# A four-layer graph network on one core: layer 3's features turned by DRAM, layer 2's by VectorE and ScalarE, in a newly searched order

## The chip, the cores and the metric

The kernel runs on one core of a Trainium2 chip. Its time is the device time of the whole execution in microseconds (us). The profile is one execution, recorded by the hardware profiler.

## What is computed

There are 32 graphs of 512 nodes with 256 features each. Each graph goes through four layers; after each layer the input is added and every node's row is normalised:

```python
x = _layernorm(x + _L0_gnn_ref(x, adj, ...))      # relu((x*(1+eps) + adj @ x) @ W1 + b1) @ W2 + b2
x = _layernorm(x + _L1_gnn_ref(x, adj, ...))      # 4-head attention, edges adj > 0.5
x = _layernorm(x + _L2_gnn_ref(x, adj, ...))      # 8-head attention, scores + log(adj + 1e-6)
x = _layernorm(x + _L3_gnn_ref(x, nodemask, adj, W))
...
# layer 2
q, k, v = split_heads(x @ Wq.T), split_heads(x @ Wk.T), split_heads(x @ Wv.T)
# layer 3
intermediate = einsum('bsh,hd->bsd', matrix, W)
similarities = einsum('bsd,btd->bst', intermediate, matrix) * adj
attn = softmax(where(mask, similarities, NEG_INF)); output = einsum('bst,bth->bsh', attn, matrix)
```

All is float32. A product on TensorE needs the contracted index on the partitions. The normalised x of a layer has nodes on the partitions, so before layers 1, 2 and 3 it has to be turned to features on the partitions: 512 x 256 becomes two tiles of 128 features x 512 nodes. This turning is what the change is about.

## The kernel before

One graph is cut into steps (some 300), each given with an engine, a planned cost in us, the steps it follows, and the buffers it takes. `Plan.order` (L134) lays the steps of up to six graphs into one order, by a due time for each step (its graph's turn, less the work that follows it, plus a shift by the step's name) and by the planned costs; `Plan.run` then emits them in that order. The order is thus fixed when the kernel is built: every engine executes its own instructions in that order and waits by semaphores. The shifts, the period and the window stand in one long list of numbers in the call of `plan.run`. Buffers come from numbered stocks: "B" 13 tiles of 128 x 2048, "C" 12 of 128 x 1024, "D" 10 of 128 x 512, and "p" the 8 banks of PSUM.

The steps that matter here, by their names in the code and the lines of the profile of before:

- **Adjacency.** For graph 0 TensorE transposes it; for the others, steps `la` (L814) let SP load it in four DMAs whose runs are 32 elements long (128 bytes), so that blocks of 32 x 32 come to lie in the right place, and steps `at` (L873) let VectorE turn each block in place ("Ar" to "AT").
- **Layer 0** is `h` (hT_ps, L340 or L344), `f` (h1T_ps) and `y` (y_ps).
- **Layer 1** ends with the transposes `yt` (y_t, L1197 and L1198), the scaling `yn` (L1203), the sum and statistics `st2` (L1212, L635, L636), then the norm: VectorE `va` (L652), POOL's power `dev` (L658), VectorE `sh` (L666), and four ScalarE `r` (L681).
- **Turning**, `features_first` (L1222): four TensorE transposes of 128 x 128 to a PSUM bank (`xt`, L1234, tile xT_t), then one ScalarE copy (`xe`, L1238, tile xT), for each of the two halves of the features. Layers 2 and 3 both use it, for every graph. Layer 1 has its own, which also sums (L971, L975).
- **Layer 2.** `proj` (qT_ps, kT_ps), `values` (v_ps), eight groups of `scores` (s, L1286: four products of 32 rows each), their exponents on ScalarE (`e`, L1299), the multiplication with the adjacency on VectorE (`m`, L1308), and eight groups of `n` (o_ps, L1344). The sums of the exponents are gathered by accumulating DMAs that POOL issues (`cd`, L1319, 1 MB each; `fd`, L1372, 512 KB), each of which waits for the ones that it adds. Then `d2` (d_ps, L1391) on TensorE, the scaling on VectorE (L1427 to L1449), and `p` (o2p_ps).
- **Layer 3.** `i` (iT_ps) and `t` (tile s) both read the turned x (xT3); then L1524 on VectorE, L1530 on ScalarE, `w` (o_ps), and the last norm. The output leaves by SP (L1581).
- `product` (L337) issues a product whole, or as four of 32 columns, whichever form TensorE is in; the planner counts 0.1 to 0.2 us for a change of form.
- Two more ways to turn x are in the code but unused: `turned` (by DRAM) and `moved` (by VectorE, with or without ScalarE).

Of the kernel before, what the change touches and what calls it, by code (L numbers as in the profile page):

```python
# [9 lines left out]
F32 = mybir.dt.float32  # L10
# [6 lines left out]
P = 128  # L17
# [31 lines left out]
class Plan:  # L49
# [84 lines left out]
    def order(self, period, ahead, window, stay, rush=(), moves=(), edges=(0, (), 0, ())):  # L134


        room = {b: [(0.0, i) for i in range(n)] for b, n in self.stock.items()}
        engine, mode, out, last = {}, "", [], 0.0
        held = [{} for _ in self.steps]
        ends = [{} for _ in self.steps]  # L140
        waits = [{n: len(s.after) for n, s in steps.items()} for steps in self.steps]
        fwaits = [[len(after) for _, after in frees] for frees in self.frees]
        ready, low, opened = {}, 0, 0
        todo = [len(steps) for steps in self.steps]
        moved = dict.fromkeys((n for steps in self.steps for n in steps), 0.0)
        turn = [max(g - 1, 0) for g in range(len(self.steps))]
        for i, early in enumerate(rush):
            turn[-1 - i] -= early
        for n, far in moves:
            moved[n] += far  # L150
        lead, tail = edges[0], len(self.steps) - edges[2]
        early, late = dict(edges[1]), dict(edges[3])

        def shift(g, name):
            return moved[name] + (early if g <= lead else late if g >= tail else {}).get(name, 0.0)

        def near(low):
            fill, until, between, left, drain = ahead
            return fill if low < until else drain if low >= len(self.steps) - left else between

        def open_to(n):
            nonlocal opened
            while opened < min(n, len(self.steps)):
                for name in self.steps[opened]:
                    if not waits[opened][name]:
                        ready[opened, name] = self.ready(opened, name, ends)
                opened += 1

        open_to(window)
        while low < len(self.steps):  # L170
            found = []
            for (g, name), t in ready.items():
                s = self.steps[g][name]
                t = max(t, engine.get(s.eng, 0.0))
                into = self.EITHER.get(mode, "c32") if s.mode == "any" else s.mode
                change = self.CHANGE[into] if s.eng == "pe" and into != mode else 0.0
                for k, (kind, _, rest) in enumerate(s.take):
                    r, n = room[kind], sum(b[0] == kind for b in s.take[:k])
                    if len(r) <= rest + n:
                        break  # L180
                    t = max(t, r[n][0])
                else:
                    due = turn[g] * period - self.left[g][name] + shift(g, name) + stay * change
                    found.append((t, due, g, name, change))
            if not found:
                return math.inf, out
            first = min(found)[0] + near(low)
            _, t, g, name, change = min((due, t, *f) for t, due, *f in found if t <= first)
            s = self.steps[g][name]
            t += change  # L190
            if s.eng == "pe":
                mode = self.EITHER.get(mode, "c32") if s.mode == "any" else s.mode
            del ready[g, name]
            got = {}
            for kind, key, _ in s.take:
                got[key] = held[g][key] = (kind, room[kind].pop(0)[1])
            if s.eng:
                engine[s.eng] = t + s.us
            end = ends[g][name] = t + s.us
            last = max(last, end)  # L200
            out.append((g, name, mode, got))
            for h, n in s.then:
                waits[h][n] -= 1
                if not waits[h][n] and h < opened:
                    ready[h, n] = self.ready(h, n, ends)
            for k in s.frees:
                fwaits[g][k] -= 1
                if not fwaits[g][k]:
                    key, after = self.frees[g][k]
                    kind, i = held[g].pop(key)  # L210
                    free = max(ends[g][a] + self.HOP.get(self.steps[g][a].eng, 0.0) for a in after)
                    room[kind].append((free, i))
                    room[kind].sort()
            todo[g] -= 1
            while low < len(self.steps) and not todo[low]:
                low += 1
                open_to(low + window)
        return last, out
# [12 lines left out]
def fast_path(  # L231
# [23 lines left out]
    nc = tc.nc  # L255
# [339 lines left out]
    def graph(g):  # L595
        plan.graph()
        slot = plan.slot[-1]
        last = g == B - 1
        t = {"g": g}
# [102 lines left out]
        def turned(n, more, src):  # L702

            @step(f"xw{n}i", "sp", 0.45, row(f"r{n}", NC))
            def _():
                t[f"xd{n}"] = dram.tile([N, D], F32, tag=f"x{n}_dram", name=f"x{n}_dram_{g}")
                nc.sync.dma_start(t[f"xd{n}"].rearrange("(c p) d -> p c d", p=P), t[src][:, :, :D])

            transfer(f"xw{n}", 2.0, (f"xw{n}i",), land=6.0)

            for a in range(4):

                @step(
                    f"xl{n}{a}i", "sp", 0.66, (f"xl{n}{a-1}i",) if a else (f"xw{n}",),
                    take=() if a else (f"C=xL{n}/{2 if n == 1 else 1}",) + more,
                )
                def _(a=a):
                    if a == 0:
                        t[f"xL{n}"] = mid(f"xL{n}", [P, DC, N], f"xL{n}")
                    nc.sync.dma_start(  # L720
                        t[f"xL{n}"][32 * a : 32 * a + 32].rearrange("j d (b i) -> j d b i", i=32),
                        bass.AP(
                            t[f"xd{n}"].tensor, t[f"xd{n}"].offset + 32 * a,
                            [[D, 32], [P, DC], [32 * D, N // 32], [1, 32]],
                        ),
                    )

                transfer(f"xl{n}{a}", 1.0, (f"xl{n}{a}i",), land=5.0)

            for d in range(DC):  # L730

                @step(
                    f"xe{n}{d}", "dve", 0.66, row(f"xl{n}", 4) + prev(f"xe{n}", d),
                    take=() if d else (f"C=xT{n}",),
                )
                def _(d=d):
                    if d == 0:
                        t[f"xT{n}"] = mid(f"xT{n}", [P, DC, N], f"xT{n}")
                    nc.vector.transpose(t[f"xT{n}"][:, d, :], t[f"xL{n}"][:, d, :])

            plan.free(f"xL{n}", row(f"xe{n}", DC))

        def moved(n, more, src, shared):
# [17 lines left out]
            for b in range(4):  # L761

                @step(
                    f"xe{n}{b}", "act" if shared else "dve", 1.35 if shared else 1.3,
                    (row(f"xu{n}", DC) if shared else row(f"r{n}", NC)) + prev(f"xe{n}", b),
                    take=() if b else (f"C=xT{n}",) + more,
                )
                def _(b=b):
                    if b == 0:
                        t[f"xT{n}"] = mid(f"xT{n}", [P, DC, N], f"xT{n}")  # L770
                    to = slice(32 * b, 32 * b + 32)
                    for a in range(4):
                        of = slice(32 * a, 32 * a + 32)
                        out = t[f"xT{n}"][to].rearrange("j d (c a i) -> j d c a i", c=NC, a=4)[:, :, :, a, :]
                        if shared:
                            nc.scalar.copy(
                                out, t[f"xU{n}"][of].rearrange("j d (c b i) -> j d c b i", c=NC, b=4)[:, :, :, b, :]
                            )
                            continue
                        for d in range(DC):  # L780
                            nc.vector.transpose(out[:, d], t[src][of, :, d * P + 32 * b : d * P + 32 * b + 32])
# [458 lines left out]
        features_first(2, ("L2",))  # L1240
        bias_steps(3, row("xt2", DC))

        def proj(n, o):
            @step(
                f"{n}{o}", "pe", 1.72, row("xe2", DC) + prev(n, o) + (f"^we{n}",),
# [13 lines left out]
        def values(c):  # L1259
            @step(  # L1260
                f"v2{c}", "pe", 0.86, row("xe2", DC) + prev("v2", c) + ("^wev",),
# [230 lines left out]
        features_first(3, ("L3",), src="x3")  # L1492
# [589 lines left out]
```

## Time and profile before

| | before |
|---|---|
| median of 3 runs | 2782.68 us (2781.85 to 2784.01) |
| the profiled execution | 2784.18 us |
| its span, first to last instruction | 2782.4 us |
| mean granted clock of TensorE | 0.994 |
| busy: TensorE, VectorE, ScalarE, POOL | 2739.6, 2123.4, 1738.6, 476.5 us |
| TensorE's weight loads, beside its products | 1368.5 us |
| DMA queue of POOL (q0), share of 16 engines | 52.2% |
| DMA queue of SP (q1), share of 16 engines | 17.9% (303,296 packets) |

A line of a group reads: line of the code, engine, operation, tile written and tiles read, shapes, count, then busy time in all and mean length of one in ns, then the idle time of the engine just before these instructions and what ended it. The length of an instruction is not its price: on one engine instructions overlap, and the distance from one start to the next is shorter.

A line of a timeline reads: start in us, length, engine (with q: its sequencer, which only issues), line, operation, tiles, shapes, count of equal ones in a row.

### The profile page before, as it was taken

The numbers are of one execution on the slowest core, as the hardware profiler recorded it, in microseconds if no ns is written. First come the engines' busy times: TensorE is split into PE (matmuls) and PEld (weight loads), VectorE is DVE, ScalarE is ACT, GpSimd is POOL, SyncE is SP. The second block draws the span as 40 slices with busy tenths as digits, with TensorE's granted clock in tenths as the row PEclk, the third lists the DMA queues.
The fourth block names the chain that finished last, engine by engine and source line by source line (L and its number), as shares of the span: only waits on it lengthen the run. The fifth ranks groups of instructions, "written<-read, shape, count | busy, mean of one in ns | idle before, by whom it ended". The sixth has DMA issues, their size and how long they took to land.

```text
span 2782.4 us, 64791 instructions
## 1 busy us (share of the span) xinstructions
PE 2739.6 (98%) x27204; PEld 1368.5 (49%) x27204; DVE 2123.4 (76%) x4203; ACT 1738.6 (62%) x3374; POOL 476.5 (17%) x526
## 2 busy tenths in 40 slices
PE   8999999999999999999999999999999998999998
PEld 6545345545454445454455554455554443454434
DVE  3878778877778877778877778877778867468975
ACT  3665766667566667566666565666565655466763
POOL 1121211111122111121111121111221111111110
PEclk9999999999999999999999999999999999999999
DMA  8496787677778676777676777677787776927660
GB/s 165 88 172 128 149 175 134 138 150 141 147 146 159 136 151 137 156 137 163 135 151 138 156 143 157 136 151 142 151 149 150 143 151 118 174 52 154 135 126 25
DMA packets 350146, 390.24 MB, mean 140 GB/s; under 512 B 265036, under 2 KB 304920, under 8 KB 317976
## 3 DMA queue, kind: packets, MB, share of 16 engines
q0 software_dynamic: 45568, 277.89, 52.2%
q1 hardware_dynamic: 303296, 107.86, 17.9%
q8 instruction: 216, 3.54, 0.5%
q14 instruction: 82, 0.67, 0.1%
q10 hardware_dynamic: 984, 0.28, 0.1%
HBM read 141.38 MB, written 17.08 MB: 57 GB/s over the span
## 4 chain that ended last, share of the span: by engine, by line
PE 94%; DVE 2%; ACT 1%; DMA 1%; issue 1%; POOL 0%; ACTq 0%; DVEq 0%; POOLq 0%
PE s L1286 9%; PE o_ps L1344 8%; PE o_ps L1130 7%; PE o_ps L344 7%; PE s L344 7%; PE y_ps L340 7%; PE hT_ps L344 6%; PE v_ps L340 6%; PE h1T_ps L340 5%; PE qT_ps L344 3%; PE kT_ps L344 3%; PE iT_ps L344 3%; PE h1T_ps L344 2%; PE o2p_ps L344 2%; PE xT_t L1234 2%; PE v_ps L344 2%
## 5 line engine op out<-in xcount | busy, mean ns | idle before, releaser
L1308 DVE SCALAR_TENSOR_TENSOR z<-AT,z 128x1024 f32<-128x1024 f32 x512 | 614.2, 1212 | 228.4 <-ACT z L1299 227.9
L1299 ACT ACTIVATE z<-s 128x512 f32<-128x512 f32 x1024 | 550.2, 604 | 198.7 <-PE s L1286 151.1
L1319 POOL DMA_DIRECT2D z<-z x186 | 165.2, 890 | 1357.9 <-PE o_ps L1344 434.8
L681 ACT ACTIVATE x<-x,shift,rstd 128x256 f32<-128x256 f32 x508 | 274.2, 594 | 180.1 <-DVE shift L666 173.2
L1097 ACT ACTIVATE z<-R_bc,nT,S 128x512 f32<-128x512 f32 x512 | 377.2, 810 | 6.2 <-DMA z<-z 3.1
L1108 DVE SCALAR_TENSOR_TENSOR z<-z,T,edge 128x512 f32<-128x512 f32 x512 | 347.5, 744 | 12.0 <-ACT z L1097 11.8
L1286 PE MATMUL s<-qT,kT 32*128 32x512 f32 x2048 | 280.9, 629 | 0.0
L658 POOL TENSOR_TENSOR rstd<-ve,nhalf 128x4 f32<-128x4 f32 (+1 forms) x131 | 164.5, 1257 | 577.0 <-DVE ve L652 566.0
L1344 PE MATMUL o_ps<-z,v 128*32 128x512 f32 x2048 | 257.7, 597 | 1.3 <-DVE z L1308 1.3
L1130 PE MATMUL o_ps<-z,v 128*32 128x512 f32 x2048 | 240.7, 598 | 9.7 <-DVE z L1108 9.7
L1158 DVE TENSOR_TENSOR z<-z 128x512 f32<-128x512 f32 (+1 forms) x256 | 233.6, 950 | 3.9 <-PE o_ps L1130 2.7
L635 DVE BATCH_NORM_STATS2 st<-x 128x6 f32<-128x256 f32 x508 | 211.4, 416 | 10.1
L344 PE MATMUL o_ps<-x,z 128*32 128x257 f32 x3648 | 213.7, 380 | 0.0
L344 PE MATMUL s<-iT,xT 128*32 128x512 f32 x1744 | 196.2, 597 | 0.0
L340 PE MATMUL y_ps<-w_sb,h1T 128*128 128x256 f32 x864 | 191.1, 379 | 0.0
L340 PEld LDWEIGHTS y_ps<-w_sb,h1T 128*128 128x128 f32 x864 | 163.9, 190 | 23.0 <-issue 0.7
L344 PE MATMUL hT_ps<-AT,x 128*32 128x384 f32 (+2 forms) x2496 | 173.5, 379 | 0.0
L1286 PEld LDWEIGHTS s<-qT,kT 32*128 32x128 f32 x2048 | 92.0, 183 | 165.5 <-issue 69.6
L344 PEld LDWEIGHTS o_ps<-x,z 128*32 128x32 f32 x3648 | 117.3, 110 | 106.5 <-issue 34.8
L1530 ACT ACTIVATE z<-z,node_off 128x512 f32<-128x512 f32 x128 | 92.0, 720 | 114.7 <-DVE z L1524 114.7
L340 PE MATMUL h1T_ps<-hT,w_sb 128*128 128x512 f32 x340 | 155.5, 593 | 0.4 <-DVE rd L1190 0.4
L1130 PEld LDWEIGHTS o_ps<-z,v 128*32 128x32 f32 x2048 | 66.1, 110 | 159.1 <-issue 136.0
(187 smaller groups left out, 3893.4 us busy)
## 6 DMA issues: line engine op xcount, KB each, us to landing
z<-z POOLq DMA_DIRECT2D x186, 1024.0 KB, 8.1
x<-biases POOLq DMA_DIRECT2D x96, 512.0 KB, 10.7
R_bc<-R_dram SPq DMA_DIRECT2D x32, 1024.0 KB
Ar<-in_adj_dram SPq DMA_DIRECT2D x124, 256.0 KB
z<-z POOLq DMA_DIRECT2D x62, 512.0 KB, 9.3
x<-in_x_dram SPq DMA_DIRECT2D x32, 512.0 KB
out_dram<-x SPq DMA_DIRECT2D x31, 512.0 KB
xs_row<-xs_dram SPq DMA_DIRECT2D x32, 128.0 KB
```

The costliest lines, as they stand in the source:

```text
L340: nc.tensor.matmul(out, lhsT, rhs, start=start, stop=stop)
L344: nc.tensor.matmul(out[part], lhsT[:, part], rhs, start=start, stop=stop)
L635: nc.vector.bn_stats(t[f"st{n}"][:, c, :], t["xo" if n == 4 else "x"][:, c, :D])
L681: nc.scalar.activation(t[into][:, c, :D] if into else xn, xn, AF.Identity, bias=t[f"shift{n}"][:, c : c + 1], scale=t[f"rstd{n}"][:, c : c ...
L1097: nc.scalar.activation(t[f"e{h}"][:, c, :], t["Rbc"][:, h, :], AF.Relu, bias=t["nT"][:, h, c : c + 1], scale=t["S"][:, h, c : c + 1],)
L1108: nc.vector.scalar_tensor_tensor(z, z, t["T"][:, h, c : c + 1], t["edge"][:, c, :], op0=ALU.add, op1=ALU.mult)
L1130: nc.tensor.matmul(po[32 * q : 32 * q + 32, :], t["v"][:, c, hp * P + 32 * q : hp * P + 32 * q + 32], t[f"e{2*hp+q//2}"][:, c, :], start=( ...
L1158: nc.vector.tensor_add(z[:, :m, :], z[:, :m, :], z[:, m : 2 * m, :])
L1286: nc.tensor.matmul(pk, t["k"][hs, o, blk(c)], t["q"][hs, o, :], start=True, stop=True)
L1299: nc.scalar.activation(t[f"E{k}"][:, j, :], t[f"ps{k}{j}"], AF.Exp, scale=QSCALE)
L1308: nc.vector.scalar_tensor_tensor(z, t["AT"][:, c, None, :].to_broadcast([P, 2, N]), ADJ_EPS, z, op0=ALU.add, op1=ALU.mult,)
L1344: nc.tensor.matmul(t[f"n{o}"][32 * j : 32 * j + 32, :], t["v2"][:, c, o * P + F2 * j : o * P + F2 * (j + 1)], t[f"E{k}"][:, j, :], start=( ...
```

## The change

For graphs 2 to 28 (`near` is false) the turning changes; graphs 0, 1, 29, 30 and 31 keep `features_first`.

- **Layer 2** uses `moved(..., shared=True)`: two VectorE transposes of 128 x 512 turn every block of 32 x 32 within its 32 partitions (x to "xU"), then sixteen ScalarE copies of 32 partitions x 256 elements move the blocks between the four groups of 32 partitions (xU to xT2). The projections follow the last copy. The step that adds the next layer's bias to x by DMA follows the VectorE transposes instead of TensorE's.
- **Layer 3** uses `turned`: SP writes x3 to DRAM (512 KB, 1,024-byte runs on the SBUF side), waits for that, and reads it back in four DMAs with 128-byte runs into "xL"; two VectorE transposes then turn the blocks into xT3. The change also gives the DRAM copy another layout ([128, 4, 256] in place of [512, 256]), and adapts the reading and the transposes.
- **The order** is another one throughout. The list of numbers is replaced by a longer one, with shifts of some graphs' own (`own`). Every engine's order differs, for all graphs.
- A VectorE variant of `moved` is rewritten too, but is not used.

```diff
-    def order(self, period, ahead, window, stay, rush=(), moves=(), edges=(0, (), 0, ())):
+    def order(self, period, ahead, window, stay, rush=(), moves=(), edges=(0, (), 0, (), ())):
...
+        own = {g % len(self.steps): dict(far) for g, far in edges[4]}
...
+            some = early if g <= lead else late if g >= tail else {}
+            return moved[name] + some.get(name, 0.0) + own.get(g, {}).get(name, 0.0)
...
+        near = g < 2 or g >= B - 3
+        XE2 = DC if near else 4
...
-                t[f"xd{n}"] = dram.tile([N, D], F32, tag=f"x{n}_dram", name=f"x{n}_dram_{g}")
-                nc.sync.dma_start(t[f"xd{n}"].rearrange("(c p) d -> p c d", p=P), t[src][:, :, :D])
+                t[f"xd{n}"] = dram.tile([P, NC, D], F32, tag=f"x{n}_dram", name=f"x{n}_dram_{g}")
+                nc.sync.dma_start(t[f"xd{n}"], t[src][:, :, :D])
...
-                        t[f"xL{n}"] = mid(f"xL{n}", [P, DC, N], f"xL{n}")
+                        t[f"xL{n}"] = mid(f"xL{n}", [P, NC * DC, P], f"xL{n}")
                     nc.sync.dma_start(
-                        t[f"xL{n}"][32 * a : 32 * a + 32].rearrange("j d (b i) -> j d b i", i=32),
+                        t[f"xL{n}"][32 * a : 32 * a + 32].rearrange("j k (e i) -> j k e i", i=32),
                         bass.AP(
                             t[f"xd{n}"].tensor, t[f"xd{n}"].offset + 32 * a,
-                            [[D, 32], [P, DC], [32 * D, N // 32], [1, 32]],
+                            [[NC * D, 32], [P, NC * DC], [32 * NC * D, 4], [1, 32]],
                         ),
                     )
...
-                    nc.vector.transpose(t[f"xT{n}"][:, d, :], t[f"xL{n}"][:, d, :])
+                    nc.vector.transpose(
+                        t[f"xT{n}"][:, d, :].rearrange("p (c f) -> p c f", c=NC),
+                        t[f"xL{n}"].rearrange("p (c d) f -> p d c f", d=DC)[:, d],
+                    )
...
-        features_first(2, ("L2",))
-        bias_steps(3, row("xt2", DC))
+        if near:
+            features_first(2, ("L2",))
+            bias_steps(3, row("xt2", DC))
+        else:
+            moved(2, ("L2",), "x", True)
+            bias_steps(3, row("xu2", DC))
...
-                f"{n}{o}", "pe", 1.72, row("xe2", DC) + prev(n, o) + (f"^we{n}",),
+                f"{n}{o}", "pe", 1.72, row("xe2", XE2) + prev(n, o) + (f"^we{n}",),
...
-        features_first(3, ("L3",), src="x3")
+        if near:
+            features_first(3, ("L3",), src="x3")
+        else:
+            turned(3, ("L3",), "x3")
```

The copies and transposes of `moved`, which was there before and is now called:

```python
nc.vector.transpose(t[f"xU{n}"][:, d, :].rearrange("p (c f) -> p c f", c=NC), t[src][:, :, blk(d)])   # d = 0, 1
...
nc.scalar.copy(out, t[f"xU{n}"][of].rearrange("j d (c b i) -> j d c b i", c=NC, b=4)[:, :, :, b, :])  # b, a = 0..3
```

## The prediction

> **What bounds the kernel now.** I read the page first: its busy line, then its chain.
>
> ```profile
> PE 2739.6 (98%) x27204; PEld 1368.5 (49%) x27204; DVE 2123.4 (76%) x4203; ACT 1738.6 (62%) x3374; POOL 476.5 (17%) x526
> PE 94%; DVE 2%; ACT 1%; DMA 1%; issue 1%; POOL 0%; ACTq 0%; DVEq 0%; POOLq 0%
> ```
>
> TensorE is busy 98% of the span and holds 94% of the chain. Next the pieces of the chain in order of time (start, length), and the busy times of two stretches of 84 us:
>
> ```profile
> 1021.23 6.93 PE hT_ps L344 x160
> 1105.16 6.93 PE hT_ps L344 x160
> 1189.08 6.93 PE hT_ps L344 x160
> ```
>
> ```profile
> 1021.00:1105.00 84.00, 84.00 (x864) 42.44 (x858) 66.46 (x132) 53.88 (x106) 14.92 (x16) 1.00 0.73 147
> 1105.00:1189.00 84.00, 84.00 (x862) 42.50 (x858) 66.47 (x131) 53.99 (x106) 14.90 (x16) 1.00 0.74 147
> ```
>
> The same product starts every 83.92 us, and in the stretch (columns: PE, PEld, DVE, ACT, POOL, clock, DMA share, GB/s) PE is busy all 84.00 us at clock 1.00, DVE 66.5, ACT 53.9, DMA 74%. The middle of the kernel is one repeated period of one graph, and its length is TensorE's work alone. The list of waits agrees: PE's sum to 28 us in the whole run, most at the ends. So work taken off TensorE shortens every period, as long as no new wait takes its place.
>
> **What goes from TensorE.** Layers 2 and 3 lose their transposes (L1234) for graphs 2 to 28: 27 graphs x 2 layers x 8 = 432 instructions. What does one cost? PE's timeline:
>
> ```profile
> 1062.43 1.04 PE L1234 MATMUL xT_t<-ident,x 128*128 128x128 f32 x8
> 1063.40 1.06 PE L1344 MATMUL o_ps<-z,v 128*32 128x512 f32 x8
> ...
> 1077.33 0.60 PE L1234 MATMUL xT_t<-ident,x 128*128 128x128 f32 x4
> 1077.77 2.84 PE L340 MATMUL v_ps<-wg_sb,xT 128*128 128x264 f32 x12
> ```
>
> Four take 1077.77 - 1077.33 = 0.44 us from start to next start, 0.11 each. Their group's mean is 280 ns, and the Trainium skill (TensorE: Matmul & The Clock Gate, Part 4: PE-mode transpose) gives about 275 ns for one in a kernel. By that the saving would be 432 x 0.275 = 119 us. But those are lengths of overlapping instructions; the next starts after 0.11, so I take 432 x 0.109 = 47.1 us.
>
> The eight at 1062.43 take 0.97, 0.09 more than 8 x 0.11, because the next product uses 32-column pieces: a change of array form. Counted in the built orders, before has 536 such changes and after 460 (in the repeated period 15 and 12). 76 x 0.093 = 7.1 us. Full and quartered forms of one product cost the same (y_ps: 6.91 us as x32 and as x128). Sum: 54.2 us; per period 16 x 0.109 + 3 x 0.093 = 2.02 us, so 83.92 becomes 81.9.
>
> **What VectorE gets.** Per changed graph two 128x512 transposes for layer 2 (L764) and two for layer 3. Nearest row, L873: 678 ns (0.59 between starts). 4 x 0.68 = 2.7 us: 66.5 becomes 69.2 of 81.9, 84%. Not the bound. The strided reads have no row; from 0.59 to double, 1.2, DVE would still hold 71 of 82.
>
> **What ScalarE gets.** Sixteen copies of 32 partitions x 256, for two evacuations of 594 ns in each layer.
>
> ```profile
> L681 ACT ACTIVATE x<-x,shift,rstd 128x256 f32<-128x256 f32 x508 | 274.2, 594 | 180.1 <-DVE shift L666 173.2 <-issue 6.6 <-ACT kT L1257 0.2
> L1273 ACT COPY v<-v_ps 128x256 f32<-128x256 f32 x128 | 48.3, 378 | 6.0 <-PE v_ps L344 4.2 <-PE v_ps L340 1.6
> L873 DVE STREAM_TRANSPOSE AT<-Ar 128x512 f32<-128x512 f32 x124 | 77.9, 678 | 12.9 <-DMA Ar<-in_adj_dram 12.9
> ```
>
> Plain 256-element copies (L1273) are 378 ns long and follow each other at 0.27; the nearest with SBUF input (L681, two per-partition operands more) is 594 long. The planner's cost is 1.35 for four, 0.34. I take 0.34, nearest to the plain copy: 5.4 us. Ends: 0.27 (4.3) and 0.59 (9.5). ACT: 53.9 - 1.9 + 5.4 = 57.4 of 81.9. Not the bound, but the copies lie in a chain.
>
> **The room of layer 2.** In after's repeated order TensorE has, between the last y_t transpose and the first kT product, two h1T, two score groups, four o_ps groups, two y pairs and two iT: 3.4 + 2.1 + 3.4 + 6.9 + 3.4 = 19.3 us with changes. In before the stretch from the last y_t (1053.7) to the end of the normalised x (1062.1) took 8.3 us. The new order puts about 2.3 us more in front (a stats pair 0.6, an L1308 piece 1.2, an exponent 0.5). Then 1.4 for transposes, 5.4 for copies, 0.4 for hand-overs: 17.8. It fits with 1.5 us to spare, so I cost it at nothing; above 0.43 us per copy it stops fitting. Also queued behind the copies on ACT are iT's evacuations and the next norms; TensorE needs those 1 to 2 us later.
>
> **The DMAs of layer 3.** On SP's queue each changed graph adds one write (512 KB) and four reads of 128-byte runs (4,096 packets). SP's and POOL's timelines:
>
> ```profile
> 1055.38 0.39 SPq L1581 DMA_DIRECT2D out_dram<-x  x1
> 1055.93 15.02 SPq L814 DMA_DIRECT2D Ar<-in_adj_dram  x4
> ```
>
> ```profile
> 1052.96 0.93 POOL L1319 DMA_DIRECT2D z<-z  x1 [1.64 <-DVE z L1308]
> 1062.98 0.92 POOL L1319 DMA_DIRECT2D z<-z  x1 [3.18 <-DMA z<-z]
> 1071.43 0.87 POOL L1372 DMA_DIRECT2D z<-z  x1 [2.29 <-DMA z<-z]
> ```
>
> The adjacency's load is the same pattern at double size: 8,192 packets issued in 15.0 us beside accumulations. Half is 7.5 us, with the write in front (up to 8 beside an accumulation) and two landings of 2 to 3: about 20 us. A rule speaks against this: the Trainium skill (VectorE: DVE Perf Modes, The three transpose paths) says that a plain DMA that transposes by strides is 19 times slower than the hardware's own where the innermost stride is large; with 261 GB/s for that one (DMA: Bandwidth & Descriptors, Latency and other measured facts) 512 KB would take an estimated 38 us, and xL would come some 26 us late in every graph, and the kernel would be far slower. The row decides: here 32 elements stay together, only blocks move, and Ar shows the price.
>
> The room: from the end of o2p to iT TensorE has 42 us. Before x3 is done DVE has the sum, four statistics and fourteen L1108 pieces (0.66 from start to start), 11 us, then POOL's power and a shift, 2 (L658, L666), and ACT four L681, 2. That puts x3 at 15 and xL at 35, while DVE's turn for xT3 comes at about 36. Behind that on DVE in order stand layer 2's transposes and two L1308 pieces, so a late xL holds these; some 2 us late still reaches TensorE as nothing. SP itself blocks for the write's landing with the next adjacency load behind it, which is needed over 20 us later. POOL's bias add waits for DVE instead of TensorE; nothing hangs on it.
>
> DMA's share: in the stretch of Ar, 8,784 packets of SP's queue took 49.3% of 16 engines in 20 us; 4,608 more cost about 5.2 us of all engines, so 62 of 84 becomes 67 of 82, 82%.
>
> **Stall that could take the place.** The score sums go through three accumulations in line (issues 1052.96, 1062.98, 1071.43, the last landing 6.8 later): 25.3 us until d_ps at 1082.37 may start, with 4 to spare. In after, from the o_ps group that the first waits for (the last but one) to d_ps, TensorE has o_ps, iT, kT, s3, qT, v and four score groups, 27.2 us by their lengths in the timeline. Room falls to about 2 us, with DMA busier.
>
> **Rivals.** (1) *Contention.* Layer 3's packets lengthen an accumulation or xL, and d_ps or kT waits about 1 us in each of some 22 similar periods: 2731 + 22 = 2754. For: q0 takes 52% already, landings range from 6.8 to 10. Against: layer 3's packets fall in the other half of the period from the three accumulations. (2) *The copies* (the other side). At 0.594 each, as L681, sixteen take 9.5 us, 2.6 more than fit; every one of 27 graphs' kT waits 2.6 and 54 us turn to 2728 + 27 x 2.6 = 2799, slower. It decides from (6.9 + 2.02)/16 = 0.56 us. Against: L681's extra length goes with its two operand columns. (3) *Nothing comes of it*: the ends, with a new order and longer chains per graph, idle 54 us more than 28: 2783.
>
> **Numbers.** The profiled execution is 2784.18 (span 2782.4 and 1.8 around it), 1.5 above the median 2782.68. 2784.2 - 54.2 = 2730.0, as a median 2728.5; the margins of 1.5 to 2 us at three places will not hold in every period, an estimated 0.15 us in 22: 2732. Chances: forecast 0.64, (1) 0.23, (2) 0.08, (3) 0.05. A measurement of this kernel can tell 0.2%, 5.6 us. Range 2722 (ends idle 10 less) to 2768 (1.6 us per period lost).
>
> **Right or wrong.** The period between hT_ps starts: 81.9 if all is hidden. PE waits near 28 us; new rows "d_ps <- DMA z<-z" or "xT3 <- DMA xL" mean (1); kT_ps waiting for ACT xT, and a copy group over 430 ns between starts, mean (2). xT_t of L1234's successor should be x80. A period of 83 or more would make the forecast wrong.

## The result and the profile after

| | median, us (range) | against before, ratio [95%] |
|---|---|---|
| before | 2781.85 (2780.15 to 2784.01) | |
| after | 2765.11 (2760.23 to 2768.8) | 0.9941 [0.9926, 0.9955] |
| after, measured again with a later experiment | 2768.05 (2765.27 to 2773.57) | 0.9954 [0.994, 0.9968] |

The change makes the kernel 0.6% faster, some 17 us (0.5%, 14 us, by the mean of the two ratios); the forecast was 50. The profiled execution of after takes 2768.17 us with a span of 2766.3, 16.1 less than before's 2782.4. The busy line and the chain's line of its page:

```profile
PE 2698.4 (98%) x30888; PEld 1280.3 (46%) x30888; DVE 2178.8 (79%) x4311; ACT 1867.9 (68%) x3698; POOL 475.9 (17%) x526
PE 72%; DVE 12%; ACT 6%; DMA 5%; issue 3%; SPq 1%; POOL 0%; ACTq 0%; DVEq 0%; POOLq 0%
```

TensorE is as busy as before (98%), yet it holds 72% of the chain where it held 94%. So in places something else now ends last. The chain of after in order of time, at three of its repeated pieces (start, length):

```profile
808.45 6.91 PE y_ps L346 x128
858.30 8.03 DVE z L1116 x12
890.77 6.91 PE y_ps L346 x128
940.63 8.03 DVE z L1116 x12
973.10 6.91 PE y_ps L346 x128
```

The period is 890.77 - 808.45 = 82.32 us, down from 83.92, and a run of VectorE's stands in each of these pieces (in others, from 1100 to 1400 us and behind 1924, the chain shows TensorE alone). In the busy times of a stretch (columns as in the prediction) the engines have what was forecast: VectorE 68.0, ScalarE 58.4, DMA 82 and 87%.

```profile
1021.00:1103.00 82.00, 81.75 (x1006) 37.64 (x1002) 67.96 (x135) 58.44 (x117) 15.07 (x16) 1.00 0.84 162
1103.00:1185.00 82.00, 81.91 (x1010) 39.02 (x1002) 68.00 (x134) 58.54 (x118) 15.05 (x16) 1.00 0.87 163
```

The lists of what TensorE waits for (line, releaser: us in total, times, the longest) tell most. Before, its head:

```profile
PE o_ps L1130 <- DVE z L1108: 9.7, 3, 4.4
PE AT_t L846 <- DMA A<-in_adj_dram: 5.5, 1, 5.5
PE hT_ps L340 <- DVE ATd L852: 3.6, 1, 3.6
```

and after:

```profile
PE iT_ps L346 <- DVE xT L743: 7.5, 1, 7.5
PE R_t L1036 <- ACT R L1019: 6.9, 2, 6.0
PE d_ps L1176 <- DVE z L1166: 4.4, 14, 1.2
PE AT_t L854 <- DMA A<-in_adj_dram: 4.2, 2, 3.9
PE v_ps L346 <- ACT xT L983: 3.8, 1, 3.8
...
PE kT_ps L346 <- ACT xT L783: 3.0, 2, 1.8
...
PE qT_ps L342 <- ACT xT L783: 2.6, 2, 1.7
PE d_ps L1408 <- DMA z<-z: 2.2, 1, 2.2
```

Without the first load (AT_t), all rows sum to 28 us before and 54 after. Only the row of d_ps at L1176 (14 times) belongs to the repeated periods; the others are nearly all single waits at the two ends. Two products carry the name d_ps: the one at L1176 is layer 1's (step `d1`, at L1168 before), which reads what VectorE's additions at L1166 leave; the one at L1408 is layer 2's (step `d2`), which waits for POOL's accumulations.

The rows leave out what a wait does to the instructions behind it. I cut both spans at the R_t product (one per graph) of the seventh and of the twenty-sixth graph. TensorE's own work in each stretch is the sum of its instructions in their order, each at its usual time from start to next start; what is left of the stretch is lost time. Work and lost time are therefore estimates, good to some 3 us.

| stretch, us | before: time, work, lost | after: time, work, lost | change in work, in lost |
|---|---|---|---|
| fill, to the seventh R_t | 494.4, 464.5, 29.9 | 510.1, 463.3, 46.8 | -1.2, +16.9 |
| 19 periods | 1595.1, 1594.6, 0.5 | 1565.0, 1556.2, 8.8 | -38.4, +8.3 |
| drain, to the end | 692.9, 647.6, 45.3 | 691.2, 633.2, 58.0 | -14.4, +12.7 |

The work fell by 54.0 us, as forecast (54.2); it is priced from start to start as the forecast was, so the check that stands by itself is the period of run 5 below. Of the 54.0, 37.9 were lost again: 8 in the periods, 30 at the ends.

A wait can cost more than its row says, because the granted clock can fall behind it. Here are the product behind after's longest wait and the clock (third column from the end) before it and behind it, then the same product in run 11, where the wait is gone:

```profile
2312.23 5.94 PE L346 MATMUL iT_ps<-xT,w_sb 128*32 128x512 f32 x32 [7.53 <-DVE xT L743]
2303.30:2310.10 6.80, 1.40 (x28) 0.58 (x20) 0.00 (x0) 0.00 (x0) 0.00 (x0) 1.00 0.75 142
2310.10:2316.90 6.80, 4.67 (x24) 1.19 (x28) 4.82 (x13) 0.58 (x1) 0.22 (x1) 0.50 0.74 247
```

```profile
2308.94 3.64 PE L346 MATMUL iT_ps<-xT,w_sb 128*32 128x512 f32 x32 [0.78 <-DVE xT L1532]
```

At half the clock the product takes 5.94 us instead of 3.64, so this wait of 7.5 us costs 9.8. The same is seen at R_t: from 2240 to 2262 us the mean clock is 0.84 in after and 1.00 in run 10, where the wait is gone. It does not tell after from before, though: in both, the mean clock is 0.99 in the fill, 1.00 in the periods and 0.98 in the drain.

### The profile page after: what moved, and what is told of

It reads as the page before. It is cut to its first block, busy times and chain, and to the rows that moved or that the text cites. A ratio compares the mean times of both kernels' runs of the same rounds, so it can differ in the third digit from the quotient of the medians.

```text
span 2766.3 us, 72980 instructions
## 1 busy us (share of the span) xinstructions
PE 2698.4 (98%) x30888; PEld 1280.3 (46%) x30888; DVE 2178.8 (79%) x4311; ACT 1867.9 (68%) x3698; POOL 475.9 (17%) x526
## 4 chain that ended last, share of the span: by engine, by line
PE 72%; DVE 12%; ACT 6%; DMA 5%; issue 3%; SPq 1%; POOL 0%; ACTq 0%; DVEq 0%; POOLq 0%
PE s L1303 8%; PE y_ps L346 7%; PE o_ps L1361 6%; PE v_ps L346 5%; PE s L346 5%; DVE z L1116 4%; PE o_ps L1138 4%; PE o_ps L346 4%; DVE z L1166 4%; PE h1T_ps L342 4%; PE iT_ps L346 3%; PE h1T_ps L346 3%; ACT z L1105 3%; PE hT_ps L346 3%; PE qT_ps L342 2%
## 5 line engine op out<-in xcount | busy, mean ns | idle before, releaser
L1316 ACT ACTIVATE z<-s 128x512 f32<-128x512 f32 x1024 | 539.3, 611 | 99.0 <-PE s L1303 90.0
L1361 PE MATMUL o_ps<-z,v 128*32 128x512 f32 x2048 | 261.3, 597 | 0.5 <-DVE z L1325 0.5
L1138 PE MATMUL o_ps<-z,v 128*32 128x512 f32 x2048 | 247.0, 596 | 2.1 <-DVE z L1116 1.7
L1549 DVE TENSOR_TENSOR z<-s,AT 128x512 f32<-128x512 f32 x128 | 88.3, 690 | 189.5 <-PE s L346 119.8
L1166 DVE TENSOR_TENSOR z<-z 128x1024 f32<-128x1024 f32 (+1 forms) x256 | 232.5, 949 | 2.2 <-PE o_ps L1138 2.2
L346 PE MATMUL y_ps<-w_sb,h1T 128*32 128x256 f32 x3648 | 202.1, 379 | 0.0
L783 ACT COPY xT<-xU 32x256 f32<-32x256 f32 x432 | 173.9, 403 | 35.8 <-DVE xU L764 30.9
L939 ACT ACTIVATE h1T<-h1T_ps,b_sb 128x512 f32<-128x512 f32 x128 | 88.1, 688 | 142.6 <-PE h1T_ps L342 84.0
L346 PE MATMUL s<-iT,xT 128*32 128x512 f32 x1600 | 180.6, 593 | 0.7 <-ACT iT L1533 0.7
L346 PEld LDWEIGHTS o_ps<-x,z 128*32 128x32 f32 x3616 | 128.3, 110 | 93.6 <-issue 23.0
L346 PEld LDWEIGHTS y_ps<-w_sb,h1T 128*32 128x32 f32 x3648 | 118.6, 110 | 90.6 <-issue 10.5
```

What stands on the lines that cost most here:

```text
L346: nc.tensor.matmul(out[part], lhsT[:, part], rhs, start=start, stop=stop)
L783: nc.scalar.copy(out, t[f"xU{n}"][of].rearrange("j d (c b i) -> j d c b i", c=NC, b=4)[:, :, :, b, :])
L1138: nc.tensor.matmul(po[32 * q : 32 * q + 32, :], t["v"][:, c, hp * P + 32 * q : hp * P + 32 * q + 32], t[f"e{2*hp+q//2}"][:, c, :], start=( ...
L1166: nc.vector.tensor_add(z[:, :m, :], z[:, :m, :], z[:, m : 2 * m, :])
L1316: nc.scalar.activation(t[f"E{k}"][:, j, :], t[f"ps{k}{j}"], AF.Exp, scale=QSCALE)
L1361: nc.tensor.matmul(t[f"n{o}"][32 * j : 32 * j + 32, :], t["v2"][:, c, o * P + F2 * j : o * P + F2 * (j + 1)], t[f"E{k}"][:, j, :], start=( ...
```

## The experiments

Three theories. **T1**: in the first and last graphs the longer chains of the new turning (sixteen copies in layer 2, the DRAM trip in layer 3) aren't covered, and TensorE waits for them. **T2**: the newly searched order is the loser, in work that the turning doesn't touch. **T3**: layer 3's packets stretch all other transfers. Each run was timed beside before on its chip; its ratio is compared with after's, of which I take the mean of the two measurements, 0.9948. One interval is about 0.0015, 4 us, wide to each side, so a difference from after of less than some 5 us is not clear by the times alone. Line numbers in the kernels with an edited order are a few higher than after's.

**1. Other source.** Layer 3's reads take the graph's input x from DRAM, so they don't need the write of x3. The output is then not the reference's.

```
-  t[f"xd{n}"].tensor, t[f"xd{n}"].offset + 32 * a,
+  x.tensor, x[g].offset + 32 * a,
```

> Layer 3's four reads take their 512 KB from the graph's input x, which lies in DRAM from the start, instead of from the copy of x3 that was just written; the write stays, so order, traffic and queues are the same, only the wait for the write's landing is gone (the output is then not the reference's). Theory 1 (in the first and last graphs the longer chains of the new turning aren't covered, and TensorE waits for them): the 7.8 and 2.4 us that TensorE loses before the iT products of graph 25 go, 6 to 10 us less than after, the steady period stays at 82.3. Theory 2 (the newly searched order is itself the loser at the ends): no change, within 2 us. Theory 3 (the packets of layer 3 stretch everything else): no change either, since all packets are still there.

Measured 0.9942 [0.9928, 0.9957]: nothing, and iT's wait is still 7.2 us. T1's number failed. The chain through after's drain, SP's own timeline there, and SP's in the repeated period (the three lines from 1037.59) show why:

```profile
2286.29 1.72 PE o_ps L1361 x16
2288.00 1.19 PE s L1303 x8
...
2291.52 14.15 SPq L724
...
2305.71 5.63 DMA xL<-x_dram
...
2311.47 0.72 DVE xT L743
...
2312.23 6.00 PE iT_ps L346 x32
```

```profile
2275.66 0.57 SPq L711 DMA_DIRECT2D x_dram<-x  x1
2289.26 19.71 SPq L724 DMA_DIRECT2D xL<-x_dram  x4
```

```profile
1037.59 0.57 SPq L711 DMA_DIRECT2D x_dram<-x  x1
1043.72 6.37 SPq L724 DMA_DIRECT2D xL<-x_dram  x4
1050.34 5.80 SPq L822 DMA_DIRECT2D Ar<-in_adj_dram  x4
```

In a period the reads start 6.1 us after the write and are issued in 6.4. In the drain they start 13.6 us after it, because xL takes one of the 12 buffers that it shares with kT, qT and others, and this one is set free by a score product that ends at 2289.19. The four issues then last 19.7 us: their 128-byte packets ran from 2293.77 to 2310.70, in a stretch (2285 to 2312) with 448 packets of 8 KB on POOL's queue, which are the score sums' accumulations. The trip took 35 us there. In this experiment SP's waits name the same buffer:

```profile
SPq L724 <- PE s L1303: 18.5, 2, 13.0
```

So the wait for the write that I removed was covered by another.

**2. No DMA in layer 3.**

```
-  nc.sync.dma_start(t[f"xd{n}"], t[src][:, :, :D])      (and the four reads)
...
-  t[f"xL{n}"].rearrange("p (c d) f -> p d c f", d=DC)[:, d],
+  t[src][:, :, blk(d)],
```

> Layer 3's write and its four reads are left out; VectorE's two transposes read x3 directly, so that the blocks are not moved between quadrants (not the reference's output). Order and all other work as after. Theory 1: as the run with the other source, 6 to 10 us less than after, a little more where the trip also delays graphs 2 to 5. Theory 3: clearly more than that, 15 to 25 us less, with the steady period below 82.3 and the adjacency's loads shorter. Theory 2: within 2 us of after.

The blocks are then not moved between the groups of 32 partitions. Measured 0.9922 [0.9908, 0.9936], 7 us less than after. The period stays at 82.34, although DMA's share falls from 84 to 77%: T3 is out for the periods. The drain takes 675.9 us instead of 691.2: iT's wait is gone, and R_t's falls from 6.9 to 1.3, since the adjacency's loads no longer stand behind the trip on SP's queue. Not all of it stays won: set beside after's, the trace gains 9.9 us at iT and gives 6.6 back at the o_ps products that follow. The fill takes 512.9, no less than in after.

**3. Two plain copies in layer 2**, in place of the sixteen; the blocks are not moved.

```
+  if shared:
+      if b < DC:
+          nc.scalar.copy(t[f"xT{n}"][:, b, :], t[f"xU{n}"][:, b, :])
+      return
```

> Layer 2's sixteen ScalarE copies of 32x256 are replaced by two plain 128x512 copies, so that the blocks are not moved between quadrants (not the reference's output); the order is the same. ScalarE gets some 4 us per graph back. Theory 1: the waits of kT and qT for the copies in graphs 2, 3, 4, 26 and 27 (2.1, 1.8, 0.7, 1.4 and 2.0 us of lost time) go, 5 to 9 us less than after; steady period unchanged at 82.3. Theory 2: at most 2 us less. If the copies cost something in every period after all, some 8 us more than that.

Measured 0.9929 [0.9917, 0.9942], 5 us less than after, at the edge of what the timing tells. The waits of kT and qT for the copies are gone from the list. In the fill, 2.0 and 1.8 us won at two kT products are given back 10 and 29 us later; in the drain 1.4 are given back at R_t, whose wait grows from 6.0 to 7.6, and 1.9 stay. The period is 82.23, 0.1 shorter.

**4. Neither chain.** Runs 2 and 3 together.

> Both chains shortened: no DMA trip in layer 3 and two plain copies in place of sixteen in layer 2 (blocks are not moved in either layer, not the reference's output), in after's order. Theory 1: the sum of the two single runs or somewhat more, 12 to 20 us less than after, and the idle time of the ends comes near that of before. Theory 2 (the order itself): most of the loss stays, under 6 us less than after, and the stalls that stay have causes that have nothing to do with the turning of x.

Measured 0.9904 [0.989, 0.9919], 12 us less: the low end of T1. But by stretches the gain is in the drain (681.2 instead of 691.2) and not in the fill: 510.5 us to the seventh R_t against 510.1. With both chains shortened, the fill's 17 us are all still there.

**5. The next graph's first h1T product in front of layer 1's d_ps in the periods.** (The step `f0` is h1T's; what was expected calls it hT.) The planner's list has one entry ahead of graph 0, so 6 stands for graph 5.

```
+  for g in range(6, 27):
...
+      i, j = at[g, "d1"], at[g + 1, "f0"]
...
+          made.insert(i, made.pop(j))
```

> After with one exchange in the written order, in the repeated graphs 6 to 26: the next graph's first hT product (f0) is put in front of the attention sum d_ps (d1) instead of behind it. No work is added or taken away. In after TensorE waits about 0.4 us at d_ps in each of some 20 periods for VectorE's last addition of the exponents (L1166), because the planner put d_ps that much too early. If this wait is a matter of the order: period 82.33 becomes 81.9, and the kernel 7 to 8 us faster than after. If VectorE's chain is a bound by itself, TensorE waits the same 0.4 somewhere else, and the time stays within 2 us.

Measured 0.9921 [0.9906, 0.9936], 7.5 us less than after. The repeated pieces of its chain:

```profile
807.09 6.91 PE y_ps L352 x128
855.55 6.93 PE hT_ps L352 x160
889.05 6.91 PE y_ps L352 x128
```

The period is 81.96, VectorE's run has left these pieces of the chain, and d_ps's row has fallen from 14 waits to 2, both outside the 19 periods. After and this run, around that product:

```profile
1041.25 1.93 PE L346 MATMUL o_ps<-x,z 128*32 128x257 f32 x32
1043.43 1.08 PE L1176 MATMUL d_ps<-z,pick 128*32 128x128 f32 x32 [0.25 <-DVE z L1166]
```

```profile
1039.26 2.01 PE L352 MATMUL o_ps<-x,z 128*32 128x257 f32 x32
1041.00 1.99 PE L352 MATMUL h1T_ps<-hT,w_sb 128*32 128x512 f32 x16
```

In after d_ps starts 2.18 us behind o_ps, where the next product here starts after 1.74. That is 0.44 lost; over the 19 periods such delays sum to 6.2 us, and this run's 19 periods are 6.1 shorter (1558.9 for 1565.0). So the loss was a matter of the order: d_ps stood that much in front of VectorE's last additions, with other work at hand to put there. The other 2 of the 8 us aren't traced.

**6. TensorE's transposes back**, unread, eight in front of the first kT and eight in front of the first iT.

```
+  for k in range(DC * NC):
+      nc.tensor.transpose(pq[:, blk(k % NC)], t["x"][:, k % NC, blk(k // NC)], ident)
```

> After, with TensorE's eight transposes in layer 2 and eight in layer 3 issued again in the 27 graphs (into the bank of the next product, which overwrites them), beside all of the new work; nobody reads them. If what TensorE was relieved of is really saved (the 47.1 us of 432 transposes, and up to 7 for changes of the array's form): 38 to 50 us slower than after, period 84.1 to 84.4; some of the load at the ends falls into waits. If TensorE is no longer what sets the period, under 15 us.

Measured 1.0168 [1.0155, 1.0181], 61 us more than after, where 38 to 50 were expected. From its chain:

```profile
746.39 6.91 PE y_ps L346 x128
798.47 8.04 DVE z L1116 x12
830.96 6.91 PE y_ps L346 x128
```

The period is 84.57, 2.24 more than after's: two groups of eight at 1.05 and 1.02, where the prediction had 2.02 for 16 transposes and three changes of form. The 19 periods give 42 us; another 16 come in the fill, where the transposes stand in order for an x that isn't ready (kT_ps waits 6.4 us for the bias). So what was taken off TensorE is truly saved, and TensorE still sets the period.

**7. Before's list of shifts for the new steps, and 8. layer 3 alone changed under after's list.**

```
7  plan.run([<after's>])           ->  plan.run([<before's, 19 names added>])
8  if near: features_first(2, ...) ->  if True: features_first(2, ...)
...
```

> The new turning, in an order that the planner makes from before's list of shifts (steps that before didn't have get the shifts of the transposes whose place they take). The order was thus not searched for the new work. Theory 1: the steady period may be long, up to 84, and the ends as bad as in after or worse, since the chains are as long. Theory 2 (the newly searched list made the ends worse): the ends are shorter than after's, start and end together under 80 us lost against 95 in after.

> Only layer 3's turning is changed; layer 2 is turned by TensorE again, in all graphs, under after's list. TensorE gets back 216 transposes, 23.5 us and some form changes; ScalarE and VectorE get rid of the copies. By the sum of the parts: 24 to 30 us slower in TensorE's work, less the 5 to 9 us that the copies cost at the ends, so 15 to 25 slower than after. If the copies cost more than they save, faster than after.

Measured 3499.77 and 3491.69 us, ratios 1.2612 and 1.2563. Both expectations fail, and neither run tells T1 from T2: the period is 109 to 112 us, so the planner's list doesn't fit steps for which it wasn't searched. In run 7 one row alone, graph after graph, is

```profile
PE xT_t L979 <- ACT x L685: 182.0, 24, 9.1
```

What run 7 does show is that, with the same steps, an order can be worth 25% of the time. Not all of that is waiting: TensorE is busy for 3019 us instead of 2698, with a mean granted clock of 0.933 instead of 0.994.

**9. An exchange on ScalarE in the fill.** Two lines of ScalarE's timeline in after stand around the 3.8 us that v_ps waits at 87 us:

```profile
80.27 6.45 ACT L1105 ACTIVATE z<-R_bc,nT,S 128x512 f32<-128x512 f32 x9
86.61 0.58 ACT L983 ACTIVATE xT<-xT_t 128x512 f32<-128x512 f32 x1
```

The evacuation stands behind nine exponents. This is layer 1, which the change doesn't touch.

```
+  made: step xe11 of graph 1 in front of z11 of graph 0
```

> After with one exchange on ScalarE in the fill: the second evacuation of graph 1's layer-1 turning (xT, L983) is put directly behind the first, in front of nine exponents of graph 0 (L1105). In after TensorE waits 3.8 us for it at 87 us, although its transposes were done at 80. This is work that the change doesn't touch; only the order is new. Theory 2 (the fill's loss is the order's): the 3.8 us wait goes, and if the fill isn't held by something behind it, 2 to 4 us less than after. Theory 1 (the fill is held by the longer chains of layers 2 and 3): the wait goes but is given back before 300 us, no change.

Measured 0.9934 [0.9921, 0.9947], 4 us less than after, within its uncertainty. The wait is gone from the list, but o_ps now waits 3.7 us for VectorE's z. Beyond the 2.0 by which the first loads landed earlier, the trace at 91 us is 1.9 ahead of after's, and it stays so up to the seventh R_t (505.9 us). Weakly for T2: half of one wait is won, with work that the change doesn't touch.

**10. An exchange on VectorE in the drain.** VectorE's timeline in after:

```profile
2246.79 1.90 DVE L881 STREAM_TRANSPOSE AT<-Ar 128x512 f32<-128x512 f32 x3 [12.35 <-DMA Ar<-in_adj_dram]
...
2251.45 0.20 DVE L1012 TENSOR_TENSOR ab<-v,ab_off 128x32 f32<-128x32 f32 x1
```

VectorE stands 12 us for the next adjacency, and the small addition ab that TensorE needs is queued behind it.

```
+  made: at0 to at3 of graph 28 behind ab of graph 27
```

> After with one exchange on VectorE in the drain: the four adjacency transposes of graph 28 (L881) are put behind the small addition ab of graph 27 (L1012) instead of in front of it. In after VectorE stands 12 us before these transposes, because the adjacency's load (issued behind layer 3's reads and another write on SP's queue) lands late, and ab, R and TensorE's R_t of graph 27 wait behind them (R_t: 6.0 us). Expected: R_t's wait goes; since the next stall (iT of graph 25, whose data come late by themselves) takes it up if it is the same chain, between 0 and 6 us less than after, most likely 1 to 3, with the wait before iT longer by as much as is given back.

Measured 0.9927 [0.9914, 0.994], 6 us less. R_t's wait is gone (with the low clock behind it, the trace wins 7.6 us there), 1.5 are given back at the next v_ps, and the drain takes 680.9 us. iT's wait stays 6.9, so the two are separate.

**11. Graph 25's layer 3 by TensorE.**

```
+  if g != 25: (the write, the four reads, VectorE's transposes)
+  for d in range(DC):
+      nc.tensor.transpose(pq[:, blk(c)], t["x3"][:, c, blk(d)], ident)      (c in 0..3)
+      nc.vector.tensor_copy(t["xT3"][:, d, :], pq)
```

> After with graph 25 alone turned by TensorE in layer 3 again (eight transposes and two VectorE copies directly before iT, in iT's bank), without its write and four reads; everything else and the order as in after. Theory 1: the wait of iT for the DRAM trip of graph 25 (7.5 us, and 2.4 at the next product) goes and 3 to 4 us of turning in line come: 4 to 7 us less than after. Theory 2 or 3: no change within 2 us, since one graph's packets are few and the order is the same.

Measured 0.9925 [0.991, 0.994], 6 us less: one graph's DRAM trip costs what T1 said. In the trace 7.0 us are won at iT, net of the transposes put back, and 1.8 are given back.

**12. The corrections 5, 9, 10 and 11 in one kernel.**

> The four corrections in one kernel: the next graph's first hT product in front of d_ps in the repeated graphs, the ScalarE exchange in the fill, the VectorE exchange in the drain, and graph 25's layer 3 turned by TensorE. If their effects add up: 8 (periods) + 2 to 4 (fill) + 1 to 3 and 4 to 7 (drain) less than after, 2743 to 2750. If the ends give back what is taken from them, as 2755 as with the first correction alone.

Measured 2752.45 us, 0.9892 [0.9878, 0.9907]: some 15 us less than after and 30 less than before, the fastest version found, but short of the 2743 to 2750 that were expected if the effects add up: singly the four gave 23.5. Its period is 81.95, and its drain takes 683.8 us.

**13 to 17. The fill.** What is left is the fill's 17 us. The first of these is after itself once more:

> The changed kernel itself, unchanged, on the same chip as the next two, as their base and to see how much one kernel differs from execution to execution: 0.993 to 0.995 of before; the trace's first 60 us may differ by 1 to 4 us with the landing of the first loads, the repeated period not by more than 0.02 us.

Its ratio, 0.9954, is in the first table. Its fill took 515.3 us against 510.1 in the first trace: the first hT product started 1.6 us later, and three places between 250 and 360 us took 1.2 to 1.3 more each. So single fills agree to about 5 us only, and drains too: where its order is as in after, the drain takes 687.1 to 691.9 us (after, runs 9, 13, 14, 16).

```
14  made: xe11 of graph 1 in front of z11 of graph 0; xt10, xt11 of graph 4 in front of k0 of graph 3;
          n2 of graph 3 and h0, h1 of graph 5 in front of d2 of graph 2; n3 of graph 3 in front of p0 of graph 2
16  as 14, but r13 of graph 4 goes with xt10, he0 of graph 5 with h0, and h1 and n3 stay
15  14 and 5, 10, 11;      17  16 and 5, 10, 11
```

In runs 14 and 15 the last quarter of graph 4's nodes is turned before it is normalised (r13 stays behind), and h1 and n3 take their banks ahead of the steps that were to hand them on, so their output isn't the reference's. Runs 16 and 17 move r13 and the evacuation he0 along and leave h1 and n3 in place.

> After with the written order changed at three places of the fill alone, without adding or taking away work: ScalarE's second evacuation of graph 1's layer-1 turning directly behind the first; graph 4's layer-1 transposes in front of graph 3's first kT (which waits 1.2 us for the copies); graph 2's sum d_ps and its o2p behind graph 5's two hT products and two o_ps groups (d_ps waits 2.2 us for its accumulation's landing, and loses more in restarting). If the fill's loss against before is made of such places in the order: 5 to 8 us less than after, and the seventh graph's R_t at 502 to 505 instead of 510 us. If the fill is held by the latency of its chains whatever the order: the waits move to the next product and the gain is under 2 us.

> All corrections in one: the exchange in the repeated graphs, the three places of the fill, VectorE's exchange in the drain, graph 25's layer 3 by TensorE. 3 to 6 us less than with the four corrections before (0.9892 of before), 0.987 to 0.988, if the fill keeps what it is given; 0.989 if it gives it back.

> The test of the fill once more, now with every buffer handed on as in after: ScalarE's second evacuation of graph 1 directly behind the first; graph 4's layer-1 transposes (with the norm that they read) in front of graph 3's first kT; one o_ps group of graph 3 and the first hT product of graph 5, with its evacuation on ScalarE, in front of graph 2's sum d_ps. If the fill's loss is made of single places of the order: 4 to 7 us less than after (0.9947 of before as the mean of its two measurements), the seventh R_t at 503 to 506 where the first loads land as in after. If the chains of the fill are held by their latency: the waits turn up at the next products, and the gain is under 2 us.

> These three places of the fill, the exchange of hT and d_ps in the repeated graphs, VectorE's exchange in the drain and graph 25's layer 3 by TensorE in one kernel. 0.987 to 0.988 of before if the fill keeps what it gets; 0.989, as with the four corrections alone, if not.

Run 14: 0.9971 [0.9959, 0.9983], no gain; moving hT without its evacuation made a wait of its own, 5.1 us. Run 16 avoids that and gives 0.9948 [0.9935, 0.9962], the same as after, with the seventh R_t at 514.7. The waits of v_ps and d_ps and one of kT's are gone, and these stand in their place:

```profile
PE o2p_ps L354 <- ACT z L1113: 3.7, 1, 3.7
...
PE xT_t L987 <- ACT x L693: 3.5, 5, 2.0
...
PE o_ps L1146 <- DVE z L1124: 3.0, 1, 3.0
```

Runs 15 and 17 give 0.9911 [0.9896, 0.9927] and 0.99 [0.9883, 0.9917], no more than the four corrections alone. So neither shorter chains (run 4) nor single places of the order (run 16) give the fill back; but for run 9's 1.9 us, a wait that is removed turns up at one of the next products, behind another engine. What makes this fill 16 us longer than before's isn't settled. With the chains shortened and the clock the same, the order is what remains, but no run shows it. That whole order is another one, with the fourth R_t at 231.8 us instead of 208.1; a fill in before's order with the new turning couldn't be had, because the planner's list doesn't carry over (runs 7 and 8).

## Why the prediction was right or wrong

**What goes from TensorE: right.** With the stall at d_ps out of the way (run 5) the period is 81.96, where 81.9 was forecast, and run 6 puts 2.24 us back into it. The 0.11 from start to start was the number to take, not the 280 ns of the group. One count was off: in the traces the period has 15 changes of form before and 13 after, not 12, which makes 1.93 us per period instead of 2.02; 1.96 were measured. In the whole run it is 547 and 495, so 4.8 us instead of 7.1 for the changes.

**VectorE, ScalarE, DMA: right in the periods.** 68.0, 58.4 and 82 to 87% where 69.2, 57.4 and 82% were forecast. The copies' row:

```profile
L783 ACT COPY xT<-xU 32x256 f32<-32x256 f32 x432 | 173.9, 403 | 35.8 <-DVE xU L764 30.9
```

One copy is 403 ns long, and eleven in a row take 4.54 us in ScalarE's timeline (1063.65), 0.41 each, where I took 0.34: unlike the plain copies from PSUM, which start every 0.27, these don't overlap. Sixteen cost 6.6 us instead of 5.4, most of the 1.5 us to spare; the limit that I gave was 0.43, and the second rival needed 0.56. The room held, but barely. Who waited for the copies (engine, tile: us, times):

```profile
  PEld kT_ps L346: 21.6, 23
...
  PE kT_ps L346: 3.0, 2
```

TensorE itself stands twice, in graphs 2 and 3 of the fill. In 23 graphs only kT's weight load waits, 0.9 us each, behind products that still run; run 3 puts the price at 0.1 us per period. The rule that spoke against the reads (the Trainium skill, VectorE: DVE Perf Modes, The three transpose paths) would have made an estimated 38 us of each graph's reads; their 6.4 us of issue in a period show no such penalty for runs of 128 bytes, and are near the 7.5 that I took from the row of Ar.

**The stall in the periods: not where I looked.** I gave layer 2's d_ps 2 us of room and feared a late accumulation there. That room held: the row of L1408 in the list is a single wait of 2.2 us, in the fill. The stall that came is at the other d_ps, layer 1's, behind VectorE's last additions; I had put nothing there, since before had no such wait. It takes some 0.44 us in 13 of the 19 periods, 6.2 in all. That my 0.15 us in 22 periods, 3.3 in sum for any late place, covers half of it is luck. Run 5 shows that it was a place in the order.

**The failed step: "PE waits stay near 28 us".** The prediction took the saving for the whole run and proved cover only for the repeated period; for the ends it carried before's idle time over. The rows of waits came to 54 us, and by lost time the ends lost 30 us more. That was the mechanism of the third rival, at half its size and with a chance of 0.05. Of this, the drain's 13 are shown to be single waits for the most part: with the corrections 10 and 11 together (runs 12, 15 and 17) the drain takes 679.7 to 683.8 us, 8 less on average than in the five traces with after's drain. These waits are the trip of graph 25, which I had put at 20 us and which took 35 there (a buffer held by a score product, reads beside accumulations; runs 1, 2 and 11), and ab behind a late adjacency on VectorE (run 10). I had looked for xL's data to be late, and not for the buffer it is put in. The fill's 17 stay open: shorter chains don't bring them back (run 4), so the longer chains that the third rival named are not their cause as far as runs 2 to 4 go.

**Contention** as in the first rival: not there. All packets gone (run 2), the period is the same.

## What to carry to other kernels

A saving on the engine that sets the period is worth its sum in the periods; at the two ends the longer chain that pays for it can lie open, as graph 25's did here in the drain, so cost each added step a second time with the neighbours that it has there. A new tile in a shared pool waits for its buffer as well as for its data: ask which reader frees it. And after an order has been searched anew, look at every single wait of the critical engine: two exchanges in the written order, in the periods and in the drain, gave 7 and 6 us here, each by itself, where the whole change gave 14 to 17.

## What the runs showed of the hardware

- The same four reads of 128-byte runs, 512 KB, were issued in 6.4 us in a repeated period and in 19.7 us beside queued accumulations (after, at 1043.72 and 2289.26); the trip through DRAM took 35 us there.
- ScalarE's copies of 32 partitions by 256 from SBUF to another group of 32 partitions start every 0.41 us, those of 128 partitions by 256 from PSUM every 0.27. A quarter of the partitions made no copy shorter here, though the source differs too. With two plain copies of 128x512 in their place (run 3), ScalarE is 140 us less busy in the whole run, 5.2 per graph.
- TensorE's granted clock was at 0.50 behind single waits of 6.0 and 7.5 us and at 1.00 where these had been removed (runs 10 and 11); the product behind the longer one took 5.94 us instead of 3.64.
- Removing a wait of 2 to 4 us in the fill gained 0 to 2 (runs 3, 9 and 16). In the drain most of it stayed won in runs 10 and 11, but in run 2 two thirds of what was won at iT came back at the next o_ps.
- The first hT product started between 10.8 and 14.1 us in different executions, depending on when the first loads landed, and executions of one kernel lie up to 13 us apart (run 5); with five rounds a ratio is known to 0.15% only, so differences of 3 to 5 us rest on the traces.
